# New queue places for a graph-attention kernel: K weights and tiles of x loaded ahead of the adjacency, first projection behind the warming

## The chip, the cores and the metric

The kernel runs on one core of one Trainium2 chip. The metric is the device time of one execution in microseconds (us). The kernel before takes 1636.79 us, the median of three runs (1635.91 to 1638.03). The other cores of the chip are idle.

A core has five engines, each with its own instruction queue that is worked off strictly in the order written: TensorE (PE, matrix products), VectorE (DVE), ScalarE (ACT), GpSimd (POOL) and SyncE (SP, here used only to issue transfers). An instruction that waits holds up everything behind it on its engine. Sixteen DMA engines move data between HBM and the on-chip memory.

## What is computed

One layer of graph attention over 16 batches of 1024 rows with 512 features, 8 heads of 64:

```python
h = jnp.maximum(_layernorm(x), 0.0)
q, k, v = h @ Wq + bq, h @ Wk + bk, h @ Wv + bv          # (16, 1024, 8, 64) each
scores = einsum('bihd,bjhd->bhij', q, k) / sqrt(64)
scores += where(adj == 0, -1e9, 0)                       # adj is (1024, 1024), the same for every batch
out = x + einsum('bhij,bjhd->bihd', softmax(scores), v)
```

`adj` is sparse, with a few neighbours for most rows and up to some dozens for a few, and it is data: the kernel must find the neighbours itself, once, before any attention can start.

## The kernel before

**Once, at the start.** The 1024 x 1024 adjacency is loaded in eight tiles of 128 rows (512 KB each, `load_adj`). VectorE counts the neighbours of each row (`degree`, L922 and L926). The rows are then ranked by that count: `keys` (L937), `flip_row` (TensorE transposes, L948), `copy_row` (L953), `rank_of` (four tiles on VectorE, L958, four on ScalarE, L962), `ranks` (L968 to L981). The row numbers in rank order go through a table in HBM: `tell` scatters them (POOL, L1123, eight transfers), `collect` reads the table back (SP, L1134), `perm_of` makes the permutation `perm`. In parallel the neighbour lists are made (`list_of`, L1119 and L1120), scattered (`spread`, also L1123), read back (`collect`) and completed for the long rows (`long_rows`, `long_blocks`, `longest`, L1151 to L1176), which ends in `slots`/`spots`: the table `index` by which neighbours are gathered.

**The first batch's K and V.** While that runs, K and V of batch 0 are computed from rows in their natural order, since the permutation is not yet known. For each of eight tiles (the code numbers them -8 to -1): `load_x` (SP, L999, 256 KB), `stats`, `variance`, `power` (POOL, L1022), `shift`, `norm` (ACT, L1036), `flip` (four PE transposes, L1043), `unflip` (ACT, L1048), then `proj_kv` for K and for V (PE, L1056, eight matmul records each, and one for the bias, L1054; tile -8 gets its bias afterwards by `add_bias`, L1060), `evict_kv` (ACT, L1074), and `store_kv` (POOL, L1094), which scatters the rows of K and V to their rank. The bias itself needs three rounds of splitting into bf16 parts (`round` on ACT, L911 and L913, and `remain` on POOL, L916). `warm` is one tiny ScalarE operation, `warm_pe` three 128 x 512 products on zeros (L898).

**Every batch.** x is gathered by `perm` (`load_x`, POOL, L1001), its K and V are made a batch ahead of their use and stored to one of three HBM buffers (SP, L1098; V's bias of every second tile is added by VectorE in `evict_kv`, L1072). Attention goes by 14 units of 2 to 4 neighbour slots: `queries` (PE), `gather` of K and V rows (POOL, L1287; the row itself by SP, L1285), `multiply` (DVE, L1297), `score` (L1301), `exponent` (ACT, L1305), for some tiles `share` (DVE, L1310), `weigh_s` (ACT, L1331, 8 operations a slot) and `weigh_v` (DVE, L1317), `fold`/`join`/`scale` (L1336, L1343, L1391), `add_up` (PE, L1355, for the longest rows), `residual` (L1405) and `put_out` (POOL, L1408). PE makes K and V of the next batch while VectorE and ScalarE work on this one. `evict_kv` frees one of two PSUM buffers for projections.

**What sets the order.** Each operation is a method, and `planned` lists all of them with engine, what they depend on, and which ring of buffers they use. The dictionary `PLACES` gives each operation a number, by kind of batch (`'once'`, `'first'`, 0, 1, 2, 3 for batches 3 to 13, `'next'`, `'last'`), to which the batch number times `PERIOD` is added. `Plan.ordered` sorts each engine's operations by that number, and this is the engine's queue:

```python
for i in sorted(range(len(self.ops)), key=place.__getitem__):
    waiting.setdefault(self.ops[i][1], []).append(i)
```

The numbers do nothing else: an operation starts when its queue reaches it and its semaphores allow it.

Of the kernel before, what the change touches and what calls it, by code (L numbers as in the profile page):

```python
# [79 lines left out]
        zeros=(-36.04,),  # L80
        load_w=(-32.98, 26.56, 41.05,),
        load_b=(-34.71, -34.77, -35.63,),
        load_adj=(-34.13, -12.67, 14.84, -8.63, -4, -30.31, -40.96, -3.19,),
        warm=(72.43,),
        warm_pe=(-117.55,),
        setup=(-29.81, -39.03, -46.52,),
        parts_at=(-52.3,),
        round=(-79.63, -60.98, -54.84,),
        remain=(-32.93, -32.39,),
        degree=(-49.28, -33.78, -27.11, -31.42, -31.15, -39.52, -52.4, -27.14,),  # L90
        no_diagonal=(-16.67, -16.14, -16.55, -25.26, -28.16, -14.19, -16.75, -21.91,),
        keys=(-21.39,),
        flip_row=(-21.21, -20.29, -7.48, 21.35,),
        copy_row=(-14.63, -24.59, 3.27, -17.31,),
        rank_of=(-6.36, -1.98, -2.01, -2.04, -22.79, -19.62, -23.98, -24.41,),
        ranks=(1.61,),
        ends=(3.62,),
        list_of=(5.67, 19.53, 38.34, 5.48, 38.1, 5.53, 5.75, 39.41,),
        tell=(5.18, 18.67, 23.66, -13.28, 16.81, 20.2, 17.64, 1.29,),
        spread=(46.11, 47.89, 49.15, 49.52, 47.92, 43.57, 47.98, 49.06,),  # L100
        collect=(32.53, 35.81,),
        others=(37.22,),
        perm_of=(30.71,),
        spots=(51.08,),
        long_rows=(44.18,),
        long_blocks=(39.89, 41.1, 43.54, 45.16, 46.55,),
        longest=(54.37, 57.62, 57.83, 58.82, 72.88, 75.14, 75.29, 75.53, 78.7,),
        count_pieces=(79.29,),
        first_piece=(100.54,),
        owners=(90.29,),  # L110
        flip_owners=(102.83,),
        copy_owners=(161.28,),
        list_pieces=(103.12,),
        pieces=(120.33,),
        slots=(121.2,),
        add_bias=(-58.93, 0.47,),
        spread_bias=(99.05,),
        copy_bias=(91.36,),
    ),
    'first': dict(  # L120
        load_x=(57.73, 58, 59.95, 60.46, 60.64, 81.11, 85.33, 111.12,),
        stats=(39.96, 39.78, 39.93, 40.74, 42.66, 57.06, 61.89, 75.26,),
        norm=(11.73, 15.63, 30.85, 67.21, 76.55, 76.63, 84.74, 112.57,),
        flip=(23.02, 24.66, 35.36, 59.87, 113.57, 129.52, 130.02, 136.11,),
        unflip=(15.59, 33.07, 41.7, 77.88, 99.45, 99.58, 116.28, 154.19,),
        proj_kv=(34.4, 82.81, 37.32, 83.54, 68.96, 120.29, 129.19, 131.64, 132.42, 135.14, 144.16, 144.5, 144.53, 155.78,
            183.56, 155.81,),
        evict_kv=(42.75, 77.77, 68.69, 78.05, 69.58, 91.79, 100.91, 107.21, 123.84, 130.13, 137.21, 138.82, 167.64, 169.31,
            177.17, 177.14,),
        store_kv=(98.53, 137.49, 138.38, 138.76, 144.41, 184.88, 185.53, 186.25,),  # L130
        variance=(40.21, 42.32, 61.77, 75.49,),
        power=(46.56, 57.48, 78.57, 79,),
        shift=(42.83, 55.54, 75.85, 97.36,),
    ),
    0: dict(
        load_x=(47.75, 47.86, 47.95, 49.09, 70.47, 76.19, 76.93, 84.62,),
        norm=(34.87, 43.15, 74.35, 76.28, 78.41, 78.44, 85.09, 85.65,),
        flip=(49.27, 60.46, 60.66, 61.78, 90.78, 90.83, 93.83, 94.15,),
        unflip=(72.13, 72.57, 76.55, 78.12, 83.34, 85.72, 85.75, 89.74,),
        queries=(92.98, 94.65, 102.57, 102.6, 106.05, 129.43, 155.81, 158.16, 167.4,),  # L140
        gather=(44.16, 101.76, 50.03, 102.64, 103.5, 95.83, 104.89, 104.56, 50.25, 114.25, 105.78, 105.99, 100.87, 106.06,
            117.66, 117.24, 117.75, 100.49, 130.45, 122.31, 130.74, 140.91, 130.62, 105.57, 143.23, 143.09, 143.42, 147.45,
            147.2, 147.48, 147.42, 112.62, 160.97, 155.73, 157.32, 164.92, 162.34, 165.66, 155.81, 167.51, 167.46, 166.95,
            167.66, 170.78, 173.41, 172.96,),
        multiply=(81.25, 84.49, 91.16, 119.95, 120.62, 124.45, 131.35, 148.44, 164.83, 165.33, 173.65, 179.8, 183.04, 186.95,),
        score=(82.64, 85.53, 96.51, 120.43, 130.41, 130.72, 138.92, 163.02, 165.22, 169.52, 177.92, 181.82, 185.29, 192.73,),
        exponent=(93.75, 98.39, 99.95, 109.73, 114.52, 125.25, 135.64, 138.39, 146.32, 154.13, 176.08, 180.96, 200.94,
            202.51,),
        row_sums=(84.46, 88.7, 104.63, 121.17, 148.63, 165.16, 182.81, 213.94,),
        share=(85.18, 89.11, 109.19, 121.23,),  # L150
        weigh_v=(87.33, 138.83, 143.11, 161.48, 173.38, 172.25, 183.39, 187.27, 192.89,),
        weigh_s=(93.88, 98.51, 98.47, 98.43, 109.43, 109.24, 109.51, 114.46, 114.49, 124.55, 124.82, 133.91, 133.2, 127.46,
            137.59, 137.08, 142.89, 144.74, 142.51, 150.7, 148.87, 156.85, 154.46, 159.99, 171.68, 178.61, 179.13, 185.65,
            200.97, 200.91, 189.82, 202.26, 202.18, 202.1, 204.25, 204.18, 204.28,),
        fold=(88.96, 107.6, 117.56, 131.07, 132.62, 140.1, 146.69, 161.19, 161.39, 160.95, 164.7, 166.74, 166.65, 169.74,
            176.13, 169.94, 181.49, 175.62, 185.26, 187.21, 187.3, 179.78, 199.64, 201.86, 201.91, 203.72,),
        residual=(117.69, 129.43, 136.21, 149.14, 153.59, 168.9, 178.03, 226.28,),
        put_out=(117.72, 130.51, 151.27, 155.78, 164.82, 174.74, 183.87, 228.1,),
        join=(162.47, 172.28, 185.23,),
        scale=(164.75, 172.35, 185.32, 217.1,),  # L160
        copy_q=(147.03,),
        add_up=(186.05, 186.13, 190.36, 192.82,),
        more=(201.22,),
        pass_on=(187.61,),
        seen=(324.32,),
    ),
    1: dict(
        load_x=(-10.54, -10.43, -4.02, -0.93, -0.34, 7.32, 10.42, 10.64,),
        stats=(-37.43, -37.49, -16.44, -16.75, -18.68, -12.46, -3.94, 27.3,),
        norm=(-5.24, -5.04, 6.21, 10.39, 17.19, 17.23, 44.79, 56.55,),  # L170
        flip=(0.09, 3.88, 10.79, 10.82, 36.46, 59.09, 64.93, 72.34,),
        unflip=(-4.19, -4.03, 15.12, 29.41, 44.83, 47, 47.33, 74.24,),
        proj_kv=(4.08, 4.11, 7.25, 10.85, 41.88, 56.11, 62.55, 62.16, 65.55, 66.44, 68.46, 71.81, 73.14, 76.08, 78.32, 81.4,),
        evict_kv=(-1.97, 6.06, 12.81, 18.32, 32.41, 52.8, 47.42, 41.7, 49.62, 71.39, 58.78, 75.94, 76.73, 87.31, 90.46,
            103.67,),
        store_kv=(10.01, 9.76, 10.77, 33.05, 33.1, 33.14, 33.67, 44.44,),
        variance=(-22.47, -13.4, -6.08, 51.2,),
        power=(4.16, 10.53, 22.23, 51.77,),
        shift=(-21.87, 4.49, 25.85, 68.99,),
        queries=(89.31, 90.81, 94.69, 97.56, 99.04, 111.42, 113.4, 132.79, 172.99,),  # L180
        gather=(51.66, 83.24, 54.55, 83.5, 83.59, 54.77, 88.88, 90.25, 66.94, 92.38, 91.77, 92.95, 57.94, 100.47, 97.88,
            98.91, 100.64, 115.17, 127.6, 124.29, 138.5, 139.71, 134.16, 119.83, 143.21, 141.41, 141.61, 143.69, 143.42,
            143.36, 143.64, 158.15, 145.57, 145.48, 145.51, 149.42, 144.93, 150.81, 150.51, 168.87, 156.96, 155.12, 168.95,
            171, 172.21, 169.98,),
        multiply=(105.88, 106.39, 112.86, 126.01, 137.1, 136.51, 143.4, 147.49, 157.34, 157.79, 173.75, 174.58, 177.68,
            187.96,),
        score=(105.96, 108.46, 118.59, 126.15, 143.37, 145.98, 145.42, 152.81, 157.76, 166.25, 174.37, 176.66, 188.77, 192.3,),
        exponent=(109.09, 109.79, 110.87, 124.37, 124.84, 128.66, 128.89, 143.7, 147.16, 153.49, 176.48, 184.45, 186.59,
            190.72,),
        row_sums=(106.54, 108.76, 121.42, 126.28, 151.92, 166.05, 167.18, 216.1,),  # L190
        share=(108.4, 112.74, 121.45, 132.17,),
# [8 lines left out]
        join=(155.02, 160.08, 178.23,),  # L200
        scale=(156.15, 166.08, 179.32, 219.52,),
        copy_q=(153.13,),
        add_up=(187.19, 189.33, 219.44, 227.52,),
        more=(196.86,),
        pass_on=(227.72,),
        seen=(234.4,),
# [1400 lines left out]
```

## Time and profile before

| what | value |
|---|---|
| median of three runs | 1636.79 us |
| the profiled execution's own time | 1647.87 us |
| its span | 1646.2 us, granted TensorE clock 0.986 |
| busy: PE, DVE, ACT, POOL | 1580.3 (96%), 1539.2 (93%), 1442.9 (88%), 1254.6 (76%) us |
| DMA | 531.56 MB, mean 323 GB/s |
| last degree pass ends / first `tell` issued | 24.6 us / 37.85 us |
| first x gather by `perm` issued / first neighbour gather issued | 60.30 us / 100.92 us |
| last projection of the last batch issued | ends at about 1544.5 us |

The profiled execution is 11 us longer than the median of the timed runs. "Busy" counts an engine's time in instructions, not in waits for semaphores; the ends of matmuls are modelled. A row such as "PE pv L1054 <- DVE kvt L1072: 8.1, 8 times" says that TensorE stood idle for 8.1 us in all before the V projection of that line, each time until VectorE's eviction at L1072 had set its semaphore.

### The profile page before, as it was taken

How to read it: one execution, taken by the hardware profiler on the slowest of the kernel's cores; microseconds unless marked ns; L12 is line 12 of the kernel's file. 1: busy time of each engine (PE TensorE's matmuls, PEld its weight loads, DVE VectorE, ACT ScalarE, POOL GpSimd, SP SyncE). 2: the span in 40 equal slices, each digit the busy share in tenths (PEclk: the TensorE clock that was granted, in tenths of full speed). 3: DMA queues.
4: the chain of work that ended last, by engine and by line, in shares of the span. 5: the costliest groups of instructions: out<-in, count | busy, mean ns of one | idle time of the engine just before them, and what ended most of it. 6: DMA issues, size and time to landing. Idle time of an engine off the chain costs nothing. (4 is left out here: it accounts for less than half of the span.)

```text
span 1646.2 us, 19477 instructions
## 1 busy us (share of the span) xinstructions
PE 1580.3 (96%) x4196; PEld 733.9 (45%) x4242; DVE 1539.2 (93%) x2075; ACT 1442.9 (88%) x5428; POOL 1254.6 (76%) x1185
## 2 busy tenths in 40 slices
PE   7888999999999999999999999999999999999797
PEld 4444444444444444444444444444444444444233
DVE  7769999999999999999999999999999999998997
ACT  4248989999998989989898999989899898989897
POOL 3756777777878787877778788787788877777775
PEclk8989999999999999999999999999999999999989
DMA  5477989999999899999989999998999999998995
GB/s 205 153 279 275 341 317 341 333 327 317 356 346 352 316 353 336 318 352 350 352 318 344 337 331 343 352 341 313 353 331 326 350 346 346 325 338 299 346 361 198
DMA packets 149876, 531.56 MB, mean 323 GB/s; under 512 B 19052, under 2 KB 19052, under 8 KB 149752
## 3 DMA queue, kind: packets, MB, share of 16 engines
q0 software_dynamic: 109840, 390.70, 65.9%
q1 hardware_dynamic: 39912, 139.56, 22.5%
q8 instruction: 35, 0.57, 0.1%
q14 instruction: 89, 0.73, 0.1%
HBM read 429.46 MB, written 100.72 MB: 322 GB/s over the span
## 5 line engine op out<-in xcount | busy, mean ns | idle before, releaser
L1331 ACT ACTIVATE g<-g,weights 128x64 f32<-128x64 f32 x4704 | 1156.1, 338 | 59.7 <-DVE weights L1310 36.3
L1287 POOL DMA_INDIRECT g<-kv,index x608 | 627.5, 1032 | 218.9 <-issue 165.8
L1056 PE MATMUL pq<-wq,hT 128*128 128x512 f32 x1024 | 460.7, 592 | 0.8
L1056 PE MATMUL pv<-wv,hT 128*128 128x512 f32 x960 | 433.1, 594 | 0.2
L1056 PE MATMUL pk<-wk,hT 128*128 128x512 f32 x960 | 431.6, 592 | 1.4
L1301 DVE TENSOR_REDUCE weights<-g 128x32 f32<-128x2048 f32 (+2 forms) x224 | 423.6, 1892 | 1.0
L1297 DVE TENSOR_TENSOR g<-g,pq 128x1536 f32<-128x1536 f32 (+2 forms) x208 | 388.7, 1870 | 22.4 <-DMA g<-kv,index 10.1
L1056 PEld LDWEIGHTS pq<-wq,hT 128*128 128x128 f32 x1024 | 194.8, 190 | 222.6 <-issue 219.0
L1056 PEld LDWEIGHTS pv<-wv,hT 128*128 128x128 f32 x960 | 182.5, 190 | 221.5 <-issue 215.3
L1056 PEld LDWEIGHTS pk<-wk,hT 128*128 128x128 f32 x960 | 182.2, 190 | 205.9 <-issue 201.4
L1336 DVE TENSOR_TENSOR g<-g 128x512 f32<-128x512 f32 (+1 forms) x301 | 259.4, 870 | 12.7 <-issue 6.4
L1001 POOL DMA_INDIRECT x<-in_x_dram,perm x128 | 144.2, 1127 | 35.9 <-issue 31.5
L1408 POOL DMA_INDIRECT out_dram<-x,perm x128 | 135.4, 1058 | 45.1 <-issue 34.0
L1336 POOL TENSOR_TENSOR g<-g 128x512 f32<-128x512 f32 x90 | 117.9, 1318 | 21.8 <-DVE g L1336 17.3
L1317 DVE TENSOR_TENSOR g<-g,weights 128x512 f32<-128x512 f32 x143 | 112.0, 785 | 2.5 <-ACT weights L1305 2.4
L1036 ACT ACTIVATE h<-x,shift,rstd 128x512 f32<-128x512 f32 x120 | 95.4, 808 | 7.9 <-DVE shift L1026 5.6
L1043 PEld LDWEIGHTS pht<-ident,h 128*128 128x128 f32 x512 | 62.6, 142 | 74.1 <-issue 53.4
L1355 PE MATMUL acc<-g,ident 128*128 128x512 f32 x170 | 85.1, 615 | 9.1 <-ACT weights L1305 8.8
L1043 PE MATMUL pht<-ident,h 128*128 128x128 f32 x512 | 75.7, 276 | 13.0 <-ACT h L1036 11.4
L1405 POOL TENSOR_TENSOR x<-x,o 128x512 f32<-128x512 f32 x64 | 82.7, 1293 | 5.2 <-DVE o L1391 3.1
L1305 ACT ACTIVATE weights<-weights 128x32 f32<-128x32 f32 (+2 forms) x224 | 48.1, 220 | 42.6 <-DVE weights L1301 39.7
L1010 DVE BATCH_NORM_STATS2 st<-x 128x6 f32<-128x512 f32 x120 | 81.6, 680 | 2.6 <-DMA x<-in_x_dram,perm 2.6
(241 smaller groups left out, 1099.6 us busy)
## 6 DMA issues: line engine op xcount, KB each, us to landing
g<-kv SPq DMA_DIRECT2D x128, 512.0 KB
kv<-kvt SPq DMA_DIRECT2D x120, 512.0 KB
g<-kv,index POOLq DMA_INDIRECT x608
adj<-in_adj_dram SPq DMA_DIRECT2D x8, 512.0 KB
x_first<-in_x_dram SPq DMA_DIRECT2D x8, 256.0 KB
x<-in_x_dram,perm POOLq DMA_INDIRECT x128
out_dram<-x,perm POOLq DMA_INDIRECT x128
wk<-in_L_gnn_Wk_dram SPq DMA_DIRECT2D x1, 1024.0 KB
```

The source lines that it names most:

```text
L1001: nc.gpsimd.indirect_dma_start(out=X[n][:], out_offset=None, in_=x_rows, in_offset=on(ap=perm[:, t : t + 1], axis=0), element_offset=b * N * D
L1036: nc.scalar.activation(HN[n], X[n], AF.Relu, bias=shift, scale=scale)
L1043: nc.tensor.transpose(PH[n][:, c, :], hn[:, ts(c, P)], ident)
L1056: nc.tensor.matmul(pt, HT[n][:, c, :], W[name][:, c, :], start=(apart and c == 0), stop=(n != -NT and c == DC - 1))
L1287: nc.gpsimd.indirect_dma_start(out=G[i][:, s].rearrange("p j d -> p (j d)"), out_offset=None, in_=KV[b % len(KV)][:], in_offset=on(ap=inde ...
L1297: nc.vector.tensor_tensor(k, k, Q[b, t][:, None, :].to_broadcast([P, count, D]), ALU.mult)
L1301: nc.vector.tensor_reduce(weights[:, w, :], heads(G[i][:, :count, 0, :]), AX.X, ALU.add)
L1317: nc.vector.tensor_tensor(v, v, own.to_broadcast([P, n, H, HD]), ALU.mult)
L1331: nc.scalar.activation(v[:, h, :], v[:, h, :], AF.Identity, scale=weights[:, c + s, h : h + 1])
L1336: engine.tensor_tensor(v[:, 0:n], v[:, 0:n], v[:, first : first + n], ALU.add)
L1355: nc.tensor.matmul(ACC[b, home], owner_t if t < 0 else ident, v[:, s, :], start=(u == added_up(b, B, home)[0] and s == 0), stop=(u == adde ...
L1408: nc.gpsimd.indirect_dma_start(out=out_rows[t], out_offset=on(ap=perm[:, t : t + 1], axis=0), in_=X.pop(b * NT + TILES.index(t))[:], in_of ...
```

## The change

Only the numbers in `PLACES` differ (and the dictionary is one line longer, so every later line number of the kernel after is one higher). The instructions are the same in kind, count and size; the order in the five queues is new, in all parts of the program. The part of the diff with which the title deals:

```diff
     'once': dict(
-        zeros=(-36.04,),
-        load_w=(-32.98, 26.56, 41.05,),
-        load_b=(-34.71, -34.77, -35.63,),
-        load_adj=(-34.13, -12.67, 14.84, -8.63, -4, -30.31, -40.96, -3.19,),
-        warm=(72.43,),
-        warm_pe=(-117.55,),
+        zeros=(-16.2,),
+        load_w=(-19, -16.8, -15.6,),
+        load_b=(-19.6, -19.4, -19.2,),
+        load_adj=(-18.2, -17.8, -17, -17.6, -17.4, -17.2, -18, -18.8,),
+        warm=(-20,),
+        warm_pe=(-20,),
...
     'first': dict(
-        load_x=(57.73, 58, 59.95, 60.46, 60.64, 81.11, 85.33, 111.12,),
...
-        proj_kv=(34.4, 82.81, 37.32, 83.54, 68.96, 120.29, 129.19, 131.64, 132.42, 135.14, 144.16, 144.5, 144.53, 155.78,
-            183.56, 155.81,),
...
+        load_x=(75.29, 75.49, 76.69, 76.89, 78.69, 78.89, 79.29, 79.49,),
...
+        proj_kv=(75.89, 77.49, 76.29, 77.89, 76.89, 78.49, 79.09, 79.29, 86.87, 98.15, 99.79, 107.75, 135.06, 147.6, 153,
+            148.32,),
```

The queues at the start that come of it, in order (x-8 is the first tile of x, a one of the eight adjacency tiles, fl a flip, K-8 and V-8 projections, key and rank the row transposes):

```
SP before: a, x-8, x-7, zeros, bq, x-6, x-5, bv, bk, x-4, a, wk, a, x-3, a, x-2, a, a, a, a, x-1, wv, told, lists, wq
SP after:  x-8, x-7, bk, bv, bq, wk, a, x-6, x-5, a, a, a, a, a, a, a, wv, x-4, x-3, zeros, x-2, x-1, wq, told, lists

PE before: warm, fl-8, fl-7, K-8, fl-6, bias-8, K-7, fl-5, K-6, key, key, V-8, V-7, rank, bias V-8, fl-4, rank, V-6, K-5, ...
PE after:  warm, fl-8, fl-7, K-8, bias-8, K-7, fl-6, fl-5, K-6, key, key, V-8, bias, V-7, rank, rank, V-6, fl-4, fl-3, K-5, ...

ACT before: table load, norm-8, unflip-8, norm-7, round 0, norm-6, unflip-7, round 1, round 2, unflip-6, ...
ACT after:  table load, warm, norm-8, round 0, unflip-8, norm-7, round 1, unflip-7, round 2, evict K-8, norm-6, ...

POOL before, from the first tell: tell x2, store-8, tell x6, store-7, -6, -5, spread, long_rows, spread, x7, x6, ...
POOL after:   tell, store-8, tell x2, power, tell x5, store-7, spread, store-6, store-5, x7, long_rows, spread, x6, ...
```

On VectorE the two `stats` of tiles -8 and -7, their `variance` and `shift` now stand ahead of everything else, with `parts_at` before them; the `stats` of tiles -4 and -3 stand between `keys` and the first `copy_row`. In the steady batches (3 to 13) the queues differ from before in places of one to a few operations. Those on PE: the K projection of tile 6 stands behind the first `queries` of the batch instead of in front of it, `queries` of tile 1 stands between V and K of tile 4, and `queries` of the split rows stands between K and V of tile 2. On ACT, `norm` of tile 4 and `unflip` of tile 5 stand between the first `exponent` of a batch and its first `weigh_s`. In the last two batches the order is new in the same manner.

## What was predicted

> **What bounds the kernel now.** I read the page's busy table and forty slices first, then the busy times by stretch, then TensorE's waits, then the timeline of the two places at which TensorE stands still at the start.
>
> ```profile
> PE 1580.3 (96%) x4196; PEld 733.9 (45%) x4242; DVE 1539.2 (93%) x2075; ACT 1442.9 (88%) x5428; POOL 1254.6 (76%) x1185
> ...
> PE   7888999999999999999999999999999999999797
> ```
>
> TensorE is at 90% or more in all slices but the first four and two near the end. In the steady part the copies of the split queries (L1274) follow each other by 95 to 96 us, with PE busy for over 99% of it and DVE for some 97%. So TensorE sets the pace, VectorE is close behind, and a change can win only where TensorE is idle or at half clock. That is here:
>
> ```profile
> 0.00:10.00 10.00, 4.76 (x6) 1.85 (x6) 5.06 (x14) 1.28 (x1) 1.69 (x10) 1.00 0.75 249
> 10.00:20.00 10.00, 6.88 (x14) 3.65 (x15) 9.12 (x31) 5.24 (x8) 4.86 (x13) 0.50 1.03 402
> 80.00:90.00 10.00, 2.73 (x10) 2.36 (x11) 5.05 (x34) 3.31 (x6) 3.59 (x4) 0.59 0.67 263
> 220.00:240.00 20.00, 17.96 (x43) 7.82 (x43) 19.36 (x27) 16.45 (x64) 15.59 (x15) 0.91 0.87 319
> ```
>
> (busy us of PE, PEld, DVE, ACT, POOL, then granted clock, DMA share, GB/s), and in the waits:
>
> ```profile
> PE pht L1043 <- ACT h L1036: 11.4, 3, 9.4
> PE acc L1355 <- ACT weights L1305: 8.8, 1, 8.8
> PE pv L1054 <- DVE kvt L1072: 8.1, 8, 2.0
> PE pht_first L1043 <- ACT h_first L1036: 5.7, 2, 4.3
> PE pk L1054 <- ACT kvt L1074: 3.9, 4, 2.0
> ```
>
> The 5.7 us are the start. The 9.4 us are this:
>
> ```profile
> 73.19 0.59 ACT L1048 COPY hT<-pht 128x512 f32<-128x512 f32 x1 [1.68 <-remote]
> 85.92 0.59 ACT L1074 COPY kvt_first<-pv_first 128x512 f32<-128x512 f32 x1 [12.14 <-remote]
> ```
>
> ScalarE stands for 12.14 us before an eviction whose V projection ended at 74.4; no instruction of the profile releases it ("remote"). VectorE stutters over the same stretch, and TensorE, behind the norm that follows, idles from 77.85 to 87.27 and then runs at half clock until 94.15. That costs 9.42, and 2.35 more (8 transposes in 1.76 instead of 0.88, the bias 0.43 for 0.22, a projection 4.69 for 3.43): 11.8 us. The profiled execution takes 1647.87, the median 1636.79, 11.1 us less. I therefore count this stall as one of the profiled execution alone, and the timed program as without it. All sums below are gains on both.
>
> **The start, step by step.** SP's queue: in before 1 MB (an adjacency tile and two of x) is there at 5.82, when the second statistic runs; at the 402 GB/s of the next stretch 1 MB takes 2.6 us, so data land at 3.2 us + bytes ahead / 402 GB/s. After: x-8 at 3.9, x-7 4.5, wk (1.5 MB in) 7.1, first adjacency tile 8.4, last (6 MB in) 18.9, wv 21.5, x-4 and x-3 22.8. Statistics 0.87 each, variance 0.2, `power` 0.75, `shift` 0.2: `norm`-8 at about 6.9 (before 10.87). Then, by ACT's queue, norm 0.8, round 0.7, unflip 0.6, norm 0.8, so flip -7 at 10.2 and K-8 at 10.7 instead of 15.14. The bias parts are ready at about 12.5 (two `remain` of 1.16 between the rounds), before K-8 ends. At full clock K-8 takes 3.43 instead of 6.16; K-7 begins at 14.4 instead of 21.80. Then K-7, two flips and K-6 end at 22.5; before, key transposes came at 29.1.
>
> The adjacency gets 1.5 MB ahead of it instead of being mixed with 2.75 MB. VectorE needs 1.35 a degree pass: eight, two `stats` and small ones are 12.9 from 8.4, keys at 21.8 instead of 25.1. Behind `keys` the change puts two `stats`, which wait for x-3 at 22.8: the first `copy_row` at 23.9 instead of 30.17. From there to `spot_i` nothing changes (7.4 us), so the first `tell` comes at about 31.5 instead of 37.85. **POOL** then issues a transfer each 1.27 us without a break, and that is the bound of everything that needs `perm`: the first x gather has 13 issues and a `power` before it instead of 17, so 48.9 for 60.30. The first neighbour gather has the same number as before, minus 6.3. TensorE from the rank transposes on has the same 11 projections and one flip more: minus 6.5, up to the first query. wq leaves SP before the tables instead of behind them (75.95), 1 MB less beside the x gathers: nothing counted, since in both it is there before `queries`; SP's waits for told and lists hold only neighbour copies. `zeros` moves from 2.6 behind six tiles, to some 23, still before the first store at 32. `warm` on ACT takes 0.4 and the table load 1.28, both before x-8 lands: nothing; if x came first, 1.7.
>
> **Clock.** Row: the warming ends at 7.47, PE idles 4.26 and the next stretch has 0.50. The Trainium skill (TensorE: Matmul & The Clock Gate, Part 1) says that the clock is halved after an idle window of some 3.4 us. By it the idle pieces after the change (0.7 and 1.6 us) leave the clock full. But the row at 220:240 has 0.91 with one idle piece of 2.04 us (228.58 to 230.62), so part of a window is enough: one halved window costs 1.7. By the rule the start gains 6.5, by the row 4.8 at worst. The 1.6 us piece is nearer to pieces at 144 and 150 (1.60, 1.37), after which the clock stayed full: I take 6.5.
>
> **Steady batches.** The moved `queries` put 3.65 us between V of tile 5 and K of tile 4, as much ahead of K of tile 6, and 0.86 between K and V of tile 2. These are the projections that wait for a PSUM buffer in the 8.1 and 3.9 us; cut by that slack, those after 228 us lose 8.0 of their 11.6. But where VectorE is late TensorE may wait for it elsewhere, so 0 to 8; I take 3. Against it: ACT now meets `unflip` of tile 5 right behind `exponent`. In a batch (789.7 end of the first query) it would get there at 796.5 and PE's flip would be done at 798.3 (K 3.65, add 0.86, query 3.65, flip 0.44): a wait of 1.8, with all of `weigh_s` behind it, and `fold` and `share` of later units on DVE behind that. The cover is that ACT stood idle there anyway:
>
> ```profile
> 798.33 2.02 ACT L1331 ACTIVATE g<-g,weights 128x64 f32<-128x64 f32 x8 [2.57 <-DVE weights L1310]
> ```
>
> 2.57 us until `share`; inside it goes the wait, and two operations (1.37) leave later places. Cost 0, at most 1.8 x 14 = 25 if `share` came early.
>
> **Ramp and tail.** From 120 to 220 VectorE is busy 95.7 of 100, PE 94.2: VectorE bounds the first batches, and its first `multiply` moves with POOL, minus 6.3. `evict_kv` of batch 1's tile 7 stands right behind the first `score` on DVE: by the sums score ends at 93.6 and the V at 93.2, no wait; up to 3 if PE lags. In the tail the 8.8 us end with ACT's weighing for unit 10 of batch 14; it gets two `weigh_s` (2 x 2.0) later and the last batch's first query stands behind `pass_on`: PE idles longer, but VectorE and ACT are bound there and have the same work. 0, within 3 either way.
>
> **Sum.** Start 6.5 + steady 3 + ramp, tail 0 = 9.5 off the median: 1627.3, say **1627**. Against the profiled execution: 1647.87 - 9.5 - 11.8 = 1626.6.
>
> **Rivals.** (A) The start gains, but the first batches give it back: DVE waits for gathers, as in "DVE g L1297 <- DMA" (10.1 us over the run). Then 1634 to 1637. For it: DMA share is 0.97 to 1.00 from 100 to 120. Against: the transfers move forward with their issuer. 0.13. (B) Slower: the ACT wait at `unflip` of tile 5. It decides from the point where `share` comes within 9.1 us of the query's end (8.6 now); if half of the 1.8 falls outside the cover in 14 batches, that is 0.9 x 14 = 12.6 lost against the 6.5 of the start, with no steady gain: 1636.8 - 6.5 + 12.6 = 1643. 0.22, since small moves in eleven batches alike add up. (C) The stall at 73 to 86 is in the timed runs too and the new order avoids it: 11.8 more, 1615. Against it: the 11.1 us difference. 0.08. (D) The order gains only on PE's first projections and POOL's tells come no earlier, since x-3 or the adjacency lands late: 1634, same as A, in its chance. The forecast has the remaining 0.57.
>
> **Range and chances.** Forecast alone: 1621 (8 of steady, 1 of tail) to 1633 (halved window, no steady gain). With part of C below and most of B above: 1616 to 1643. A difference of 0.2%, 3.3 us, is about what a measurement can tell from none. Faster: forecast 0.57 and C 0.08, 0.65; same: A, 0.13; slower: B, 0.22.
>
> **What would show it.** Right: granted clock 1.0 from 10 to 20, K-8 at about 10.7, key transposes near 22.5, first `tell` near 31.5, first x gather near 49, first neighbour gather some 6 us earlier than 100.92 less the stall; fewer us in "pv L1054 <- DVE kvt". Wrong: ACT idle before `unflip` of more than 2 us in each batch, a period above 96 us, or a longer tail after the last V projection than the 102 us of now.

## The result and the profile after

| | before | after |
|---|---|---|
| median | 1636.35 us (1629.93 to 1638.03, 4 runs) | 1614.13 us (1612.02 to 1616.26, 4 runs) |
| ratio, 95% interval | | 0.9871, 0.984 to 0.990 |
| profiled execution, span | 1647.87, 1646.2 us | 1612.02, 1609.9 us |
| busy PE, DVE, ACT | 1580.3, 1539.2, 1442.9 us | 1572.1, 1518.2, 1444.8 us |
| period of a batch (products of the split queries, batches 4 to 12) | 96.14 us | 94.81 us |

The change is worth 22.2 us by these medians, 1.3%, of which 4 to 6 us do not come from the order, as far as the later runs tell; 9.5 were predicted, and the measured time lies 2 us under the low end of the range. The page of after:

```profile
PE 1572.1 (98%) x4242; PEld 732.0 (45%) x4242; DVE 1518.2 (94%) x2075; ACT 1444.8 (90%) x5428; POOL 1258.7 (78%) x1185
...
PE   8999999999999999999999999999999999999687
```

TensorE is at 90% or more from the second slice to the thirty-seventh; the weak slices at the start are gone, those near the end are not. The same stretches as in the prediction (busy us of PE, PEld, DVE, ACT, POOL, then granted clock, DMA share, GB/s):

```profile
0.00:10.00 10.00, 5.92 (x11) 2.46 (x11) 3.79 (x13) 4.49 (x7) 3.99 (x17) 1.00 0.75 257
10.00:20.00 10.00, 8.61 (x28) 4.27 (x29) 9.89 (x27) 4.73 (x8) 3.91 (x10) 1.00 1.03 411
80.00:90.00 10.00, 10.00 (x31) 4.96 (x30) 9.48 (x34) 4.18 (x7) 7.56 (x9) 0.85 0.85 294
220.00:240.00 20.00, 20.00 (x54) 9.18 (x53) 18.65 (x24) 20.00 (x82) 15.34 (x15) 1.00 0.88 308
```

The clock is full from 10 to 20 us (0.50 before), and from 220 to 240 TensorE is busy throughout. Its waits over the whole run (us in total, times, longest):

```profile
PE acc L1356 <- ACT g L1332: 10.8, 2, 9.2
PE acc L1356 <- DVE g L1337: 3.8, 1, 3.8
PE acc L1356 <- POOL g L1337: 3.7, 2, 3.5
PE pht_first L1044 <- ACT h_first L1037: 2.8, 2, 1.4
...
PE pht L1044 <- ACT hT L1049: 1.9, 1, 1.9
```

The waits of projections for an eviction ("pv <- DVE kvt", "pk <- ACT kvt", 12 us before) are gone from this trace; a second one, of after_beside below, has 4.0 us of "pk <- ACT kvt". What is left stands in the tail ("acc", the products of `add_up`).

**One count for all kernels.** TensorE has the same work in all of them and is the bound, so what an order costs can be read as time that TensorE loses. The waits view counts an idle time from the end of one matmul record to the start of the next. But records overlap: within a projection a record lasts 0.59 us and the next begins 0.43 after it. I therefore took, for each record, the time until the next one starts, less what it is without a wait (0.429 for a 128x512 product, 0.109 for a transpose, 0.216 for a bias, the medians of the trace, and 0.216 more where a bias record is missing). This also counts half clock. A few smaller products have no such measure, so the sums are good to about 1 us. In us:

| kernel | 0 to 70 | 70 to 100 | 100 to 240 | 240 to 1500 | 1500 to end | sum |
|---|---|---|---|---|---|---|
| before | 11.8 | 12.2 | 11.0 | 20.8 | 21.6 | 77.4 |
| after | 5.9 | 4.1 | 0.2 | 3.5 | 26.3 | 40.1 |

The difference is 37.3; the two spans differ by 36.3. The medians differ by 22.2 only, because the profiled execution of before is 11.5 us above its median and that of after 2.1 below: the row of before shows more loss than a median run has. The rest of the text asks how much of each column is the order's.

### The profile page after: what moved, and what is told of

Same layout as the page of the kernel before. It is cut to its first block, busy times and chain, and to the rows that moved or that the text cites. A ratio compares the mean times of both kernels' runs of the same rounds, so it can differ in the third digit from the quotient of the medians.

```text
span 1609.9 us, 19515 instructions
## 1 busy us (share of the span) xinstructions
PE 1572.1 (98%) x4242; PEld 732.0 (45%) x4242; DVE 1518.2 (94%) x2075; ACT 1444.8 (90%) x5428; POOL 1258.7 (78%) x1185
## 5 line engine op out<-in xcount | busy, mean ns | idle before, releaser
L1288 POOL DMA_INDIRECT g<-kv,index x608 | 642.2, 1056 | 206.7 <-issue 163.2
L1057 PE MATMUL pq<-wq,hT 128*128 128x512 f32 x1024 | 462.4, 595 | 0.0
L1057 PE MATMUL pk<-wk,hT 128*128 128x512 f32 x960 | 431.7, 593 | 0.0
L1057 PE MATMUL pv<-wv,hT 128*128 128x512 f32 x960 | 431.4, 593 | 0.0
L1298 DVE TENSOR_TENSOR g<-g,pq 128x2048 f32<-128x2048 f32 (+2 forms) x208 | 388.7, 1870 | 28.1 <-DMA g<-kv 9.9
L1057 PEld LDWEIGHTS pq<-wq,hT 128*128 128x128 f32 x1024 | 195.8, 191 | 216.9 <-issue 213.2
L1057 PEld LDWEIGHTS pv<-wv,hT 128*128 128x128 f32 x960 | 182.4, 190 | 213.5 <-issue 210.6
L1057 PEld LDWEIGHTS pk<-wk,hT 128*128 128x128 f32 x960 | 182.7, 190 | 201.4 <-issue 196.8
L1337 DVE TENSOR_TENSOR g<-g 128x512 f32<-128x512 f32 (+1 forms) x301 | 253.9, 851 | 9.8 <-ACT g L1332 8.4
L1002 POOL DMA_INDIRECT x<-in_x_dram,perm x128 | 135.8, 1061 | 34.9 <-issue 32.5
L1337 POOL TENSOR_TENSOR g<-g 128x512 f32<-128x512 f32 x90 | 115.0, 1284 | 17.6 <-DVE g L1337 10.5
L1037 ACT ACTIVATE h<-x,shift,rstd 128x512 f32<-128x512 f32 x120 | 96.5, 807 | 12.0 <-DVE shift L1027 11.4
L1318 DVE TENSOR_TENSOR g<-g,weights 128x512 f32<-128x512 f32 x143 | 101.9, 716 | 1.1 <-ACT weights L1306 0.6
L1049 ACT COPY hT<-pht 128x512 f32<-128x512 f32 x128 | 73.0, 571 | 16.3 <-PE pht L1044 16.2
```

Of the source, the lines that this page charges most:

```text
L1002: nc.gpsimd.indirect_dma_start(out=X[n][:], out_offset=None, in_=x_rows, in_offset=on(ap=perm[:, t : t + 1], axis=0), element_offset=b * N * D
L1037: nc.scalar.activation(HN[n], X[n], AF.Relu, bias=shift, scale=scale)
L1057: nc.tensor.matmul(pt, HT[n][:, c, :], W[name][:, c, :], start=(apart and c == 0), stop=(n != -NT and c == DC - 1))
L1288: nc.gpsimd.indirect_dma_start(out=G[i][:, s].rearrange("p j d -> p (j d)"), out_offset=None, in_=KV[b % len(KV)][:], in_offset=on(ap=inde ...
L1298: nc.vector.tensor_tensor(k, k, Q[b, t][:, None, :].to_broadcast([P, count, D]), ALU.mult)
L1318: nc.vector.tensor_tensor(v, v, own.to_broadcast([P, n, H, HD]), ALU.mult)
```

## The experiments

Both dictionaries stand in these kernels, and the queue is put together from the two orders. `ordered` takes the places as an argument; the rest of the code is that of before.

### Which stretch of the program gains: start_after, steady_after, tail_before

```diff
+    def mixed(self):
+        queue = self.ordered(self.places(PLACES_AFTER))
+        queue = queue[:queue.index(("multiply", 3 * NU))]
+        done = set(queue)
+        queue += [key for key in self.ordered(self.places(PLACES)) if key not in done]
+        rank = {key: k for k, key in enumerate(queue)}
+        return self.ordered([rank[op[0]] for op in self.ops])
```

This is start_after (after up to batch 3, then before). steady_after takes before, after from `3 * NU`, before again from `14 * NU`; tail_before takes after, then before from `14 * NU`.

> The order of after up to the first multiply of batch 3, the order of before from there on. Theory 1 (the gain comes from three places, sized by TensorE's lost time in the two profiles: start 5.9, first batches 10.8, steady batches 17, tail -4.5): about 1620, 1616 to 1625. Theory 2 (the prediction's sizes: start 6.5, nothing in the first batches): 1630. Theory 3 (the stall of 11.8 us near 73 to 86 us is in the timed runs of before as well, and its going is most of the gain): 1614 to 1618, near all of the 22 us.

> The order of before up to the first multiply of batch 3, that of after to the first multiply of batch 14, that of before again. Theory 1: 17 us less than before (period of a batch 94.7 instead of 96.2), about 1620, 1616 to 1626. Theory 2: 3 us less, 1633. Theory 3: 1632 or more; and its profile, with the start of before, would show the stall near 73 to 86 us again, which theory 1 does not expect.

> The order of after up to the first multiply of batch 14, then the order of before. Theory 1: the new order of the last two batches costs 4 to 5 us, so 1610, 1607 to 1612, which is faster than both kernels. Theory 2 (the tail counts nothing): 1614, within 1.

Measured, with before at 1638.64 on that chip: start_after 1628.22 (0.9931, 0.9911 to 0.9951), steady_after 1643.39 (1.0024, 1.0009 to 1.0039), tail_before 1630.11 (0.994, 0.9918 to 0.9961). So the order up to batch 3 gives 10.4 us, between the first theory (16.7) and the second (6.5). steady_after fits the third theory alone (1632 or more, with the stall), tail_before none, and the count says why: both lose 11 to 12 us between 1440 and 1500 us, where the two orders are joined and before and after lose 1.1 and 0.4. The seam at batch 14 spoils them; the seam at batch 3 costs nothing that can be seen (1.3 us or less from 340 to 440). And all four kernels traced on this chip, q_both below among them, had the stall near 70 to 85 us, those with the new start too (10.4 to 11.7 us lost from 70 to 100).

### Without the second seam, and after once more: later_after, after_again

later_after is before up to `3 * NU`, then after to the end.

> The order of before up to the first multiply of batch 3, then the order of after to the end, with no second seam at batch 14. Theory 1 (the steady batches and the tail give what the start, 10.4 us in start_after, does not): 22 - 10 = 12 us less than before, 1624 to 1629. Theory 2 (the steady order gives nothing by itself): 1636 to 1640.

> The kernel after once more, unchanged, beside the other kernels of this call. Theory 1 (the short stall near 70 to 85 us, 2 us instead of 9, and the steady batches without loss belong to this order): 1612 to 1617, with TensorE idle for less than 3 us between 70 and 100 us. Theory 2 (they were luck of one session, since the same order of the start in the kernel start_after had the long stall): 1620 to 1628, with a stall of 6 us or more in its profile.

Measured, with before at 1632.95: later_after 1625.24 (0.9952, 0.9936 to 0.9968), 7.7 us less where the first theory had 12; after_again 1614.63 (0.988, 0.9862 to 0.9897), 18.3 less. The 10.4 up to batch 3, from the other chip, and the 7.7 behind it make 18.1: the two parts add up to the whole. On this chip the stall was in no kernel: later_after, with the start of before, loses 0.5 us from 70 to 100, so its absence does not belong to the new order.

### The start alone and the first batches alone: first_after, head_after, ramp_after

The cut of start_after at other places: first_after at `("multiply", 0)`, head_after at `("tell", 1)`. ramp_after is before up to `("multiply", 0)`, after up to `3 * NU`, then before.

> The order of after up to the first multiply of batch 0 (the whole start), the order of before from there on. If the start is the gain and the first batches only pass it on: as much as start_after had, 10 us less than before. If the new order of batches 0 to 2 is what takes TensorE's waits between 100 and 240 us away: 3 to 6 us less than before, with 8 to 10 us lost there still.

> The order of after only up to the first tell (the loads, the first statistics, K of three tiles, the ranking), the order of before from there on. If K weights and two tiles of x ahead of the adjacency are the gain of the start, as wk_back says (11.7 us lost with the weights behind it): 7 to 11 us less than before. If the later order of tells and gathers is needed as well: 0 to 4 us less.

> The order of before up to the first multiply of batch 0 and again from batch 3 on; between them (batches 0 to 2) the order of after. If the new order of the first batches is the gain by itself (start_after gave 10, first_after with the start alone 2): 8 us less than before, 0.995. If it can only be had together with the early start, because TensorE is the bound and has no backlog to spend without it: 0 to 3 us less, 0.998 to 1.000.

Measured: first_after 0.9986 (0.9966 to 1.0005), 2 us; head_after 0.9996 (0.9978 to 1.0014), nothing; ramp_after 0.9981 (0.9963 to 1.0), 2 us. Together, in start_after, they give 10 (each against before on its own chip). Neither half does it alone. The count of first_after from 0 on is 5.7, 3.9, 9.7: the early start saves 4.8 us against before_again (10.5, 1.6, 10.0), 2.3 of it is lost again from 70 to 100 because TensorE now comes to a transpose before ScalarE has emptied its buffer, and the 10 us from 100 to 240 are lost as before. The transpose in first_after:

```profile
78.87 0.79 PE L1051 MATMUL pht<-ident,h 128*128 128x128 f32 x4 [1.91 <-ACT hT L1056]
```

In the batches from 100 to 240, before_again first, then after_again, both without the stall:

```profile
120.00:140.00 20.00, 17.22 (x47) 7.64 (x46) 19.69 (x33) 16.89 (x65) 13.61 (x14) 1.00 0.93 337
140.00:160.00 20.00, 18.82 (x50) 8.80 (x50) 18.44 (x26) 18.91 (x72) 13.60 (x14) 1.00 0.69 248
200.00:220.00 20.00, 17.96 (x48) 8.29 (x49) 19.34 (x31) 15.98 (x65) 16.24 (x17) 0.98 0.97 365
```

```profile
120.00:140.00 20.00, 20.00 (x56) 9.41 (x55) 19.55 (x42) 18.63 (x73) 15.48 (x15) 1.00 0.89 303
140.00:160.00 20.00, 20.00 (x56) 9.30 (x55) 19.56 (x26) 18.77 (x69) 16.47 (x16) 1.00 0.93 355
200.00:220.00 20.00, 20.00 (x53) 9.14 (x52) 18.90 (x32) 17.41 (x69) 16.57 (x16) 1.00 0.97 355
```

VectorE is nearly as busy in the one as in the other. TensorE is at 17.2 to 18.8 of 20 with the old order of these batches and at 20.0 with the new one. And with the new order behind the old start (ramp_after), a stretch and a wait of TensorE:

```profile
100.00:120.00 20.00, 12.91 (x39) 6.11 (x38) 9.62 (x24) 4.38 (x13) 11.32 (x13) 0.97 1.01 404
```

```profile
PE pq L1065 <- DVE g L1308: 5.8, 1, 5.8
```

TensorE stands 5.8 us before a query that needs the buffer of an earlier one, until VectorE's first multiplies have read it, and half clock follows (granted clock 0.86 from 120 to 140): 10.4 us are lost from 100 to 140 and 0.4 from 140 to 240, in sum as much as with the old order.

### The K weights: wk_back

```diff
-        load_w=(-19, -16.8, -15.6,),
+        load_w=(-16.9, -16.8, -15.6,),
```

> The kernel after, with the K weights behind the adjacency again instead of ahead of it: nothing else is moved. They land some 12 us later, so K of the first tile begins near 21 us instead of 10.5, TensorE idles for some 8 us more and falls to half clock. If TensorE's early start is what the start's gain is made of: 6 to 10 us more than after_again. If the tells and gathers of GpSimd set the pace of the start: within 3 us of after_again, since the adjacency then comes 2.6 us sooner.

1626.32 (0.996, 0.9945 to 0.9976): 11.7 us more than after_again on the same chip. TensorE waits for the weights ("PE pk_first L1057 <- DMA wk", 10.4 us) and loses 18.2 us up to 70 instead of 6.9; all of it arrives at the end of the program:

```profile
10.00:20.00 10.00, 0.34 (x4) 0.10 (x1) 9.91 (x30) 1.44 (x3) 4.46 (x12) 0.54 1.02 404
```

So in the whole new order a later start of TensorE costs its full price, although the early start put before the old order is worth 2 us. The 11.7 are not the gain over before, for wk_back starts later than before does: K of the first tile at 20.74 instead of 15.14, the first `tell` at 44.43 instead of 37.85.

### A second trace of before, and the last batch: before_again, last_before

> The kernel before once more, unchanged, with its trace, beside the kernels of this call. If the stall at 73 to 86 us belongs to this order: TensorE loses 10 us or more between 70 and 100 us, as in the first trace. If it belongs to the session (all kernels of the first call had it, none of the second): it is there or not in all four kernels of this call alike, and its time is near 1638 with it and near 1633 without it. In both cases TensorE loses some 9 to 10 us between 100 and 240 us and some 17 to 20 between 240 and 1500.

> The order of after up to the first multiply of the last batch, then the order of before. TensorE loses 26 us from 1500 us on in after, 22 in before. If the last batch's order is what costs the 4 us and the seam costs nothing: 3 to 4 us less than after, the fastest of all, 0.986 to 0.987 of before. If the seam disturbs it as at batch 14 (11 us lost in tail_before): 5 us or more above after, 0.991 or higher.

before_again took 1633.51; its count is 10.5, 1.6, 10.0, 25.5, 21.6, without the stall, as the other three kernels of this chip. The 240 to 1500 column is high here, as is the profiled execution (1641.57, the longest of its eight and 8.1 above their median). last_before is 1614.96 (0.9887, 0.9861 to 0.9913), the same as after within the interval: the old order of the last batch gains nothing.

### Which queue makes the steady gain: q_both, q_back, q_back_2, evict_early, pa_after

q_both is before with two groups of queries moved as after has them, and with the copy on ScalarE that the second group needs; q_back is after with the same two groups moved back. The third move of TensorE's queue, the first `queries` ahead of K of tile 6, is in neither: q_both does not make it, q_back leaves it. The edit of q_both:

```diff
+for b in range(3, self.batches - 2):
+    for moved, ahead in (
+        (("queries", b, 1), ("proj_kv", (b + 1) * NT + TILES.index(4), 0)),
+        (("copy_q", b), ("unflip", (b + 1) * NT + TILES.index(2))),
+        (("queries", b, -1), ("proj_kv", (b + 1) * NT + TILES.index(2), 1)),
+    ):
+        if queue.index(ahead) < queue.index(moved):
+            queue.remove(moved)
+            queue.insert(queue.index(ahead), moved)
```

> The order of before, but in batches 3 to 13 the queries of tile 1 stand ahead of K of tile 4, and the queries of the split rows ahead of V of tile 2. If these two moves are what takes the waits for an eviction away: 1.1 us a batch, 12 us less, 1624 to 1627. If the waits only move to other projections, because VectorE is the one that is late: 0 to 3 us less, 1633 to 1637.

1668.15 (1.0178, 1.0153 to 1.0203): 29.5 us more, where 12 less or nothing was expected. The waits of TensorE say where it went:

```profile
PE pht L1057 <- ACT h L1050: 22.2, 19, 9.2
...
PE pk L1068 <- ACT kvt L1088: 7.2, 7, 1.9
```

TensorE no longer waits for VectorE's evictions as long, and comes instead to the transposes before ScalarE has normalised their rows: 22.2 us (9.2 of it the stall), where before has 11.4 (9.4 of it the stall).

> The order of after; in batches 3 to 13 only the two groups of queries on TensorE go back to where before has them (tile 1 behind K of tile 4, the split rows behind V of tile 2). If these moves are what takes the waits away, as the prediction had it: 11 x 1.1 = 12 us more than after, 0.995 of before. If the other queues' places alone do it: within 3 us of after, 0.987 to 0.990.

> The kernel after, unchanged, on the same chip as q_back_2. If the ratio of after holds on any chip: 0.986 to 0.990 of before. If the long stall near 70 to 85 us (present on some chips, whatever the kernel) is there again: TensorE loses some 11 us there instead of 4, in both kernels alike, and the ratio stays.

> q_back once more (after, with only the two groups of queries on TensorE put back in batches 3 to 13), beside after on one chip. If TensorE's queries carry the steady gain: 8 to 13 us more than after_beside, with 12 us or more lost by TensorE between 240 and 1500 us beside the 4 to 5 of after. If q_back was slow by its chip: within 3 us of after_beside.

q_back was 0.9941 (0.9922 to 0.996), but on a chip on which after itself had not run. On one chip, with before at 1639.52: after_beside 1622.91 (0.9908, 0.9885 to 0.9931), q_back_2 1625.29 (0.9911, 0.9891 to 0.993). The 2.4 us between them are inside the intervals: putting the queries back costs little or nothing. Chips differ in more than the stall: from 240 to 1500 the trace of q_back loses about 20 us, that of q_back_2, the same order on the other chip, about 10, beside about 8 in after_beside.

evict_early moves two evictions of VectorE in before:

```diff
+for moved, ahead in (
+    (("evict_kv", n + TILES.index(5), 1), ("multiply", b * NU + 6)),
+    (("evict_kv", n + TILES.index(3), 1), ("multiply", b * NU + 9)),
+):
+    queue.remove(moved)
+    queue.insert(queue.index(ahead), moved)
```

> The order of before; in batches 3 to 13 only two operations of VectorE are moved: the eviction of V of tile 5 ahead of one multiply, that of tile 3 ahead of another, so that the two waits of TensorE for VectorE's eviction (0.64 and 0.46 us a batch) end earlier. If these waits are the steady loss: 11 x 1.1 = 12 us less, 0.9925. If VectorE, 97% busy, is as much a bound as TensorE: 0 to 4 us less, 0.9975 to 1.000, with the wait elsewhere.

0.9989 (0.997 to 1.0008): 1.7 us, no difference that can be measured. The waits:

```profile
PE pht L1056 <- ACT h L1049: 15.2, 8, 9.5
...
PE pv L1067 <- DVE kvt L1085: 3.7, 3, 2.0
```

The wait for VectorE's evictions falls from 8.1 to 3.7 us, and that for ScalarE's norm rises from 11.4 to 15.2 (9.4 and 9.5 of it the stall). pa_after takes two whole queues from batch 3 on, those of TensorE and ScalarE.

> As later_after, but from batch 3 on only the queues of TensorE and ScalarE are those of after; VectorE, GpSimd and SyncE keep those of before. If the moved projections and queries are the steady gain: as later_after, within 3 us. If the places of VectorE's evictions and of the gathers are: as before or slower, as in q_both, which moved two groups of queries alone and took 29 us longer.

1785.45 (1.0921): 152 us more, with waits of 55.4 us for ScalarE's norms and 53.5 for its evictions. VectorE's or GpSimd's queue alone was not tried: buffers are handed out in the order of the places, and a queue taken alone does not fit the others' order. The same misfit can be part of the 152 us.

### The feared wait of ScalarE: unflip_back

```diff
+    moved, behind = ("unflip", (b + 1) * NT + TILES.index(5)), ("weigh_s", b * NU, 0)
+    queue.remove(moved)
+    queue.insert(queue.index(behind) + 1, moved)
```

> The order of after; in batches 3 to 13 only unflip of tile 5 goes back behind the first weigh_s on ScalarE. If ScalarE's wait there costs 0.9 us a batch (the prediction's slower rival): 10 us less than after, 0.981. If it is covered, as the forecast took it: within 2 us of after, 0.987 to 0.989.

0.9923 (0.9896 to 0.9951), on the chip of q_back, where after itself did not run; after was 0.9871, 0.988 and 0.9908 on others. The 0.981 of a costly wait lies outside the interval, so as far as ratios carry over from chip to chip the wait had not cost 10 us. Whether unflip_back is slower than after stays open.

## Why the prediction was wrong, step by step

The sum had 6.5 for the start, 0 for the first batches, 3 for the steady batches and 0 for the tail. Measured were 10.4 for start and first batches together, 7.7 for all that comes behind them, and 4 to 6 that are apparently the chip's. On one chip the gain is 16.6 to 18.3, near double the forecast.

**The stall (11.8 us, "one of the profiled execution alone").** Not so, as far as the later chips tell. Every trace taken on three of them has it, whatever the kernel (9 to 12 us lost from 70 to 100), and none on two others (0.1 to 4.1). On the chips without it before takes 1632.95 and 1633.61, on those with it 1638.64, 1639.52 and 1644.74. After has it too. ScalarE in after_beside:

```profile
72.12 0.59 ACT L1075 COPY kvt_first<-pv_first 128x512 f32<-128x512 f32 x1 [4.67 <-remote]
82.09 0.81 ACT L1037 ACTIVATE h<-x,after_told 128x512 f32<-128x512 f32 x1 [9.39 <-remote]
```

In the first trace of after the same operation starts at 72.73, behind TensorE. After takes 1622.91 with it and 1614.63 without; all six runs with it (1619.82 to 1629.39, the profiled one at 1620.61) are longer than all five without (1610.84 to 1617.04). So rival C, which named 1615, has the right number by luck: timed runs on such chips are longer, but the new order does not avoid the stall. It enters the result another way. Three of the four runs of before are those shown ahead (1635.91 to 1638.03); the fourth, measured with after, took 1629.93, and after's trace has no stall. On one chip the change gives 18.3 us (after_again) and 16.6 (after_beside); the other 4 to 6 of the 22.2 are, as far as these runs tell, the chip. Whether the three runs had the stall cannot be told, since they left no trace. And the 11.1 us by which the profiled execution was longer were no proof that they had not: before_again's is 8.1 above its median without any stall.

**The start (6.5 us).** The times of its first steps were right, predicted and measured: first norm 6.9, 6.62; second flip 10.2, 9.96; K of the first tile 10.7, 10.45; of the second 14.4, 14.32; full clock from 10 to 20. From the ranking on it lagged: key transposes 22.5, 23.88; first tell 31.5, 32.93; first x gather 48.9, 53.16, because four of GpSimd's 13 issues between them took 1.4 to 1.9 us instead of 0.96, and I had counted all alike. In after:

```profile
37.00 1.37 POOL L1124 DMA_INDIRECT told_table<-before_told,spot_i  x1 [0.30 <-issue]
39.30 1.53 POOL L1124 DMA_INDIRECT told_table<-before_told,spot_i  x1 [0.19 <-POOL before_told L1023]
43.67 1.94 POOL L1124 DMA_INDIRECT told_table<-before_told,spot_i  x1 [0.30 <-DVE before_lists L1121]
50.96 1.90 POOL L1095 DMA_INDIRECT kv<-kvt_first,rank_i  x1 [0.30 <-issue]
53.16 0.98 POOL L1002 DMA_INDIRECT x<-in_x_dram,perm  x1 [0.30 <-issue]
```

Before had shown it: there the gather has 15 issues in front of it, not the 17 of the prediction, and three of them are long:

```profile
45.73 1.94 POOL L1123 DMA_INDIRECT told_table<-before_told,spot_i  x1 [0.31 <-issue]
50.51 1.95 POOL L1094 DMA_INDIRECT kv<-kvt_first,rank_i  x1 [0.30 <-issue]
56.73 1.97 POOL L1151 DMA_INDIRECT adj_long<-in_adj_dram,perm  x1 [0.30 <-DVE before_lists L1120]
60.30 0.98 POOL L1001 DMA_INDIRECT x<-in_x_dram,perm  x1 [0.30 <-issue]
```

The step that failed is "minus 6.5, up to the first query". On one chip, from before_again to first_after, the first query moves from 83.47 to 79.45 and the first neighbour gather from 89.86 to 86.91: 4.0 and 3.0 us instead of 6.5 and 6.3. And the lead is not kept to the end: alone the start gives 2 us (first_after).

**The first batches ("0, VectorE bounds them").** This is the first large miss. VectorE's 95.7 of 100 was read as a bound that no order could pass; TensorE's 94.2 beside it was the loss: 11.0 us from 100 to 240, which the new order removes nearly whole (0.2). In the same 100 us (120 to 220) of after VectorE does 96.9, and TensorE 100. With the early start it makes 10.4 us (start_after) where the two halves alone give 2 each. This interaction was not in my sum at all.

**The steady batches (3 us, at most 8).** The term was mis-sized. Behind batch 3 the change gives 7.7 us (later_after), and that is after the tail's loss. The ceiling of 8.0 came from the waits view, which shows only what exceeds the overlap of two records (a loss of 0.64 us before K of tile 4 stands there as 0.47), and nothing of shorter waits. Counted by starts, before loses 20.8 us from 240 to 1500; after loses 3.5, after_again 4.9, later_after 5.3. These differences are above the 7.7 for two reasons: the traced executions of before are slow ones, and the tail takes some back. An estimate from before_again: 25.5, less the 8.1 by which it is above its median, less 5.3, less some 4 in the tail, leaves 8. The Trainium skill (Perfetto Trace Analysis, Tensor Engine Instruction) says that a TensorE end is estimated from the size of the instruction; the overlap of 0.16 us here fits it, and starts are the safer thing to subtract.

The reason given, the moved queries, is not shown. Two of the three moved alone cost 29.5 us (q_both), moved back 2.4 by the medians, inside the intervals (q_back_2), and VectorE's evictions alone give nothing that can be measured. In q_both and evict_early the wait for VectorE that was taken away came back as waits for ScalarE. What the runs show is that none of the groups tried carries the gain; that only orders that fit each other on all queues (98, 94 and 90% busy) keep TensorE from waiting is my reading of it. Which of the places are needed stays open.

**The tail (0, within 3).** TensorE loses 26.3 us there instead of 21.6, 4.7 more, and the tail after the last V projection is 106.2 us long instead of 101.7, which the prediction had named as a sign of being wrong. last_before, with the last batch in the old order, still loses 26.2 and takes the same time: so the order of the last batch does not make it. What does stays open.

**Rivals.** A (the first batches give the gain of the start back) is what first_after shows when their order is left as it was; in the change itself it did not happen. B (ScalarE's wait at unflip) is half right: ScalarE's waits for a flip ("ACT hT <- PE pht") grow from 5.9 to 16.2 us over the run, about 1 us a batch, but no run shows that they cost anything.

## What to carry to other kernels

Where one engine is busy for nearly the whole span (96% here), size a new order by that engine's lost time, counted from start to start and by stretch, before any single wait is priced, and compare the traced execution with its median first; "another engine is at 95% too" does not make the loss zero. An early start is worth its price only if the order behind it has work that can use the lead: try a changed stretch alone and with its neighbour. When all queues are nearly full, moving one group towards a better order can cost more than the whole change gains, since a wait taken away at one engine can return at the next.

## What the hardware showed

**The stall.** On three of the five chips of the experiments, for some 13 us near 70 to 85 us, VectorE and ScalarE stand still although the profile names no other engine and no transfer that they wait for. In after_beside VectorE, between instructions that follow each other in some 0.04 us elsewhere:

```profile
72.80 0.27 DVE L1167 MAX8 adj_long<-adj_long 128x8 f32<-128x64 f32 x1 [1.78 <-issue]
...
74.21 0.09 DVE L1166 MATCH_VALUE_LOAD adj_long<-adj_long 128x8 f32 x1 [0.98 <-DVE adj_long L1165]
...
75.60 0.27 DVE L1167 MAX8 adj_long<-adj_long 128x8 f32<-128x64 f32 x1 [1.06 <-DVE adj_long L1166]
```

VectorE stands for 1 to 1.8 us, and the profile names its own earlier instruction or none. GpSimd goes on issuing a transfer every 1.27 us meanwhile, to 78.36. What causes it these runs do not show. One rival is open, a late load of instructions: the queues that the profile calls "instruction" move nothing from 67 to 82 us in after_beside and one packet each in after_again. Each chip was measured at one time only, so the chip cannot be told from the hour. After takes 8 us more with the stall (1622.91, 1614.63), before 5 to 12.

**The clock.** The same idle piece of 1.91 us near 78 us was followed by 3.4 us at half clock in after and last_before, and by none in after_again. The piece and a window behind it, in after, then in after_again:

```profile
79.08 0.66 PE L1044 MATMUL pht<-ident,h 128*128 128x128 f32 x4 [1.91 <-ACT hT L1049]
81.00:82.00 1.00, 1.00 (x2) 0.42 (x2) 0.93 (x4) 0.59 (x2) 0.97 (x1) 0.50 0.84 340
```

```profile
80.01 0.66 PE L1044 MATMUL pht<-ident,h 128*128 128x128 f32 x4 [1.91 <-ACT hT L1049]
82.00:83.00 1.00, 1.00 (x4) 0.52 (x3) 0.93 (x5) 0.53 (x2) 0.96 (x1) 1.00 0.87 352
```

So an idle piece shorter than the 3.4 us of the prediction's rule can be followed by half clock, and whether a piece of 2 us costs 1.7 us more (half of those 3.4 us) is not fixed by its length.
